# A per-sample convolution chain on one Trainium2 core: W in 18 product blocks, S2 on VectorE, the residual's identity on ScalarE, and R's shared products moved between W's

## The chip, the core and the metric

The kernel runs on one core of one Trainium2 chip. Its engines run side by side, each with its own instruction queue: TensorE (PE in the profile, its weight loads PEld) multiplies, VectorE (DVE), ScalarE (ACT) and GpSimd (POOL) work element by element, SyncE (SP) issues transfers. Products land in PSUM, eight banks of 512 fp32 columns on each of 128 partitions; everything else lives in SBUF. The metric is device time in microseconds, the median of several runs.

## The reference

A chain of four modulated 1-D convolutions, each with 64 channels in and out and three taps, on 128 samples of length 1024, and the input added at the end. Each sample has its own weights: a style vector scales the input channels, and a demodulation factor normalises the output channels.

```
s = style @ mw.T + mb
weight = SCALE * w * s[:, None, :, None]
demod = lax.rsqrt(jnp.sum(weight * weight, axis=(2, 3)) + EPS)
weight = weight * demod[:, :, None, None]
# types: 'same', 'upsample' (transposed conv, then blur), 'same', 'downsample' (blur, then stride 2)
...
x = x + _L0_cond_ref(x, cond_512, weights, biases, mod_w, mod_b)
```

Between the layers there is no nonlinearity, so for one sample the whole chain is one convolution of nine taps with a 64x64 matrix each, apart from a few columns at both ends.

## The kernel before, in words

**Tiling.** Samples are taken in 32 quads of four. A tile has 128 partitions, two samples of 64 channels, and two such halves. A "product" here is one weight block times one moving operand for all four samples: four 64x64 matmuls, one for each quarter of the array, which the profile records as 8 matmuls since each is fp32. A "block" is 64 columns.

**The chain for one quad.** scale3 makes wd (layer 3's weights, scaled per sample). stage1 multiplies by layer 2's weights and evicts S, scaled by table tB. stage2 multiplies by E (layer 1's taps with the blur) and evicts R, scaled by tC, seven blocks. stage3 multiplies by layer 0's weights and evicts W, nine blocks, scaled by t0. combine_a and combine_b on VectorE form sums of W (H, a fast-convolution scheme) and add the residual's identity to the middle tap (residual, L659). The input planes are combined alike into T. Then five convolutions, conv0 to conv4, each three groups of one 340-column product (L753), go into accumulator A (tile psA, two banks) or Y (two banks); VectorE combines them (sum1, sum2), ScalarE writes the output (L830), and SP stores it.

**Shared products.** From quad 8 on, parts of these products are computed once. stage1_a and stage1_b (L389) make S with w2n, negated taps and their sums, and VectorE's L442 and GpSimd's L445 complete it. share_sums (L462, VectorE) adds slots of S; share (L467, three products of one block) multiplies these by E into spare columns of accumulator A[q], and share_copy (L490, ScalarE) spreads them over psR, to which stage2_rest (L467, 14 products) adds. In stage3, r_sums (L588, GpSimd) adds slots of R; stage3_b (L571, 7 products into psA) ends with their product, ScalarE copies that into psW four times, and stage3_a (L571, 4 products into psW) adds the rest.

**Order.** The schedule is written by hand: each engine executes in program order. One turn q handles the convolutions of quad q, with n = q + 1, c = q + 2 and s = q + 4 in earlier stages: stage2(c), conv2(q), sum2(q), stage3_b(c), conv4(q), stage3_a(c), conv3(n), stage1_a(s), conv0(q), stage1_b(s), share(c + 1), conv1(n). Turns 0 to 3 have an order of their own (early_turn), turn 4 opens the shared form (entry), turns 5 to 28 are alike; share runs in turns 5 to 27 (sharing), and turns 10, 14, 15, 19 also carry products for the ends of the samples (SLOTS, L994). The last three quads follow in the open.

**PSUM.** All eight banks are in use: two accumulators psA of two banks (pool ps_conv), Y of two, and two single banks (pool ps_w) that psR, psW and psS take in turn; so each of these waits until the one before is evicted. In A, columns 0 to 339 of each bank hold the sums and the rest is spare; banks(q) names the two halves. sum2 is

```
m3 = m3c.pop(q)
for s, a in enumerate(banks(q)):
    sum_of(Y[:, s, :NB], m3[:, s], 3.0, a[:, :NB])
for s, a in parts(q) if 1 in steps else ():
    nc_v.tensor_sub(y1w[q][:, s], y1w[q][:, s], a)
```

that is, Y in two instructions (L662), and then y1 in one (L812), all reading A[q]. conv4 adds to Y and conv0 to A[q] afterwards. Small constants are computed in Y's spare columns; L1454 clears these.

Of the kernel before, what the change touches and what calls it, by code (L numbers as in the profile page):

```python
# [63 lines left out]
def kernel(  # L64
# [199 lines left out]
    def var_newton(bs, ls=slice(0, NL)):  # L264
# [5 lines left out]
    tA, tB, tBn, tC, t0, t3, td, tb = (  # L270
        const.tile([P, NQ, 2], F32, name=n) for n in ("tA", "tB", "tBn", "tC", "t0", "t3", "td", "tb")
# [24 lines left out]
    def table_Bn(bs):  # L296
        qs = slice(bs.start // 4, bs.stop // 4)
        nc_g.tensor_scalar_mul(tBn[:, qs], tB[:, qs], -1.0)

    def table_0(bs):  # L300
        table(nc_g, t0, bs, ALT, ODD, sc[:, 0, bs], 1.0)

# [63 lines left out]
    w2n = const.tile([P, 5, C], F32, name="w2n")  # L366

    def split_weights():
        nc_g.tensor_copy(w3x[:, :K], w3)
        nc_g.tensor_scalar_mul(w2n[:, :K], woi[2], -1.0)  # L370
        for t, src in ((w3x, w3), (w2n, woi[2])):
            nc_g.tensor_add(t[:, K:], src[:, : K - 1], src[:, 1:])
# [32 lines left out]
    EVEN = slice(0, K, 2)  # L405

    def stage1(q, pool=None, engs=(nc_a, nc_a), between=None):

        wd = chain[q]
        ps = unit(pool or ps_w, f"psS{q}")  # L410
        for k, (at, at1) in enumerate(((0, 3), (3, 1), (1, 4))):
            tap_matmul(ps, wd, at, 2, woi[2][:, k, :], EVEN, first=k == 0)
            tap_matmul(ps, wd, at1, 1, woi[2][:, k, :], slice(1, 2), last=k == K - 1)
        if between:
            between()
        st, _ = s_tiles(q)
        for r in range(2):
            scaled_copy(engs[r], flat(st[r][:, 1:6]), ps[r][:, : 5 * C], tB[:, q, r : r + 1])
        chain[q] = st
        return ps  # L420

    def stage1_a(q, ps=None):

        ps = ps or unit(ps_w, f"psS{q}")
        wd = chain[q]
        tap_matmul(ps, wd, 2, 2, w2n[:, 0, :], EVEN, first=True)
        tap_matmul(ps, wd, 3, 2, w2n[:, 2, :], EVEN)
        tap_matmul(ps, wd, 1, 1, w2n[:, 1, :], slice(1, 2))
        st, t = s_tiles(q)
        for r in range(2):  # L430
            scaled_copy(nc_a, flat(st[r][:, :4]), ps[r][:, C : 5 * C], tBn[:, q, r : r + 1])
        chain[q] = wd, ps, st, t

    def stage1_b(q):

        wd, ps, st, t = chain[q]
        tap_matmul(ps, wd, 2, 1, w2n[:, 3, :], slice(3, 4))
        tap_matmul(ps, wd, 4, 1, w2n[:, 4, :], slice(4, 5), last=True)
        for r in range(2):
            p1 = st[r][:, 0:1, :].to_broadcast([P, 2, C])  # L440
            sums = ps[r][:, 2 * C : 6 * C].rearrange("c (a b o) -> c a b o", a=2, b=2)[:, :, 0]
            nc_v.scalar_tensor_tensor(  # L442
                st[r][:, 4:6, :], sums, tB[:, q, r : r + 1], p1, op0=ALU.mult, op1=ALU.subtract
            )
        nc_g.tensor_add(t[:, :, 2], t[:, :, 2], t[:, :, 0])  # L445
# [7 lines left out]
    def tap_differences():  # L453
# [4 lines left out]
        nc_g.tensor_sub(Ed[:, 4:], E[:, 3:8:4], E[:, 5:6].to_broadcast([P, 2, C]))  # L458

    def share_sums(q):  # L460
        t = whole[q]
        nc_v.tensor_add(t[:, :, 6:8], t[:, :, 1:5:3], t[:, :, 2:6:3])  # L462
# [13 lines left out]
    def share(q, ps):  # L476

        at = [NB + 4 + i * C for i in range(3)]
        p12, p34 = ([b[:, i:j] for b in ps] for i, j in zip(at, at[1:]))
        chain_matmul(p12, E[:, 2], chain[q], slice(6, 7))  # L480
        chain_matmul(p34, E[:, 6], chain[q], slice(6, 7))
        chain_matmul(p34, E[:, 5], chain[q], slice(7, 8), True)
        shared_ps[q] = [b[:, at[0] : at[2]] for b in ps]

    def share_copy(q):

        ps = unit(ps_w, f"psR{q}")
        for r in range(2):
            src = shared_ps[q][r].rearrange("c (a o) -> c a o", a=2)
            nc_a.copy(  # L490
                ps[r][:, C : 5 * C].rearrange("c (a b o) -> c a b o", a=2, b=2),
# [4 lines left out]
    def stage2_rest(q):  # L496

        ps = shared_ps.pop(q)
        block = lambda i, n=1: [b[:, i * C : (i + n) * C] for b in ps]
        apart = [b[:, : 4 * C].rearrange("c (a b o) -> c a b o", a=2, b=2)[:, :, 0] for b in ps]  # L500
        plan = (
            (apart, E[:, 0], slice(1, 4, 2)),
            (block(1), Ed[:, 0], slice(2, 3)),
            (block(2), Ed[:, 1], slice(1, 2)),
            (block(3), E[:, 2], slice(3, 4)),
            (block(3), Ed[:, 2], slice(2, 3)),
            (block(4), Ed[:, 3], slice(1, 2)),
            (block(4), E[:, 4], slice(3, 4)),
            (block(5, 2), E[:, 8], slice(2, 4)),
            (block(5), E[:, 6], slice(3, 4)),  # L510
            (block(1, 2), E[:, 1], slice(4, 6)),
            (block(2), E[:, 3], slice(4, 5)),
            (block(3), Ed[:, 4], slice(5, 6)),
            (block(4), Ed[:, 5], slice(4, 5)),
            (block(5), E[:, 7], slice(5, 6)),
# [5 lines left out]
    def stage2(q, pool=None, engs=(nc_a, nc_a), between=None):  # L521
# [3 lines left out]
        for n, e in enumerate(() if shared else (-2, -1, 0, 1, 2, 3, 4, 5, 6)):  # L525
            if e % 2 == 0:
                a, lo, m = slice(1, 4), e // 2 + 1, 3
            else:
                a, lo, m = slice(4, 6), (e + 3) // 2, 2
            for r, rows in enumerate(HALF):  # L530
                for c, cols in enumerate(HALF):
                    src = st[c if r == 0 else 1 - c]
                    nc.tensor.matmul(  # L533
                        ps[r][cols, lo * C : (lo + m) * C],
                        E[rows, e + 2, :],
# [7 lines left out]
        t = r_pool.tile([P, 2, 9, C], F32, tag="R", name=f"R{q}")  # L543
        for r in range(2):
            scaled_copy(engs[r], flat(t[:, r, :7]), ps[r][:, : 7 * C], tC[:, q, r : r + 1])
# [4 lines left out]
    TAPS = slice(3, 9, 2), slice(4, 9, 2), slice(0, 3)  # L550

    def tap(kind, g):
        return range(9)[TAPS[kind]][g]
# [7 lines left out]
    def tap_shares():  # L561
        nc_g.tensor_sub(Wd[:, 0], woi[0][:, 0, :], woi[0][:, 1, :])
        nc_g.tensor_sub(Wd[:, 1], w0s[1][:, 2, :], w0s[1][:, 1, :])
# [16 lines left out]
    def stage3_out(q, ps, at, n, engs=(nc_a, nc_a)):  # L580
        W = Wq[q][0]
        for r in range(2):
            src = ps[r][:, : n * C].rearrange("c (a o) -> c a o", o=C)
            scaled_copy(engs[r], W[:, at : at + n, r], src, t0[:, q, r : r + 1])

    def r_sums(q, eng):
        t = chain[q]
        eng.tensor_add(t[:, :, 7:9], t[:, :, 2:6:3], t[:, :, 3:7:3])  # L588
# [3 lines left out]
    def stage3_b(q, ps):  # L592
# [16 lines left out]
        for i, f in enumerate((1.0, 1.0 / 3.0)):  # L609
            for dst, v in zip(blocks(pw, slice(i, i + 3, 2)), src):  # L610
                scaled_copy(nc_a, dst, v, f)
        stage3_out(q, ps, 0, 5)

    def stage3_a(q):
# [10 lines left out]
        stage3_out(q, pw, 5, 4)  # L625

    def stage3(q, part, pool=None, engs=(nc_a, nc_a)):
# [23 lines left out]
        stage3_out(q, ps, *((3, 6), (0, 3))[part], engs)  # L651
        return ps

    def residual(q):

        W = Wq[q][0]
        for r in range(2):
# [11 lines left out]
    def combine_a(q):  # L669
# [4 lines left out]
        residual(q)  # L674
# [91 lines left out]

# [870 lines left out]
```

## Time and profile before

| | |
|---|---|
| median of 3 runs | 480.74 us (480.36 to 481.32) |
| span of the profiled execution | 478.0 us |
| TensorE busy | 469.6 us, 98% |
| VectorE busy | 417.5 us, 87% |
| ScalarE busy | 310.1 us, 65% |
| GpSimd busy | 163.5 us, 34% |
| HBM traffic | 144 GB/s over the span |
| a turn without end products | 13.84 us |

The span runs from the first to the last instruction of one profiled execution, and the runs' time includes what lies around it. Engines overlap, so their times do not add up to the span. Rows of the profile give a line of the kernel (L753 is line 753; a line may be that of a helper), engine, operation, what is written and read, the shape, the count, the busy time and the mean of one in ns, and the idle time of the engine before it with what ended that.

### The profile page before, as it was taken

The page shows a single profiled execution, that of the slowest core. Times are in us where ns is not written, and L with a number is a line of the kernel's source. Part 1 is how long each engine was busy: PE and PEld are TensorE (multiplying, and loading weights), DVE is VectorE, ACT ScalarE, POOL GpSimd, SP SyncE. Part 2 cuts the span into 40 slices and gives each one's busy share as a digit, 9 for nine tenths or more (in the row PEclk, how much of TensorE's full clock was granted, in tenths as well). Part 3 has the DMA queues.
Part 4 walks back from the last instruction along what each step waited for, and adds up shares of the span by engine and source line. Part 5 has one row for each costly group of instructions (what it writes and reads, how often), then busy time and mean ns, then how long its engine had stood idle before and what let it go on. Part 6 is the DMA issues. An engine that isn't in the chain of part 4 may idle for free.

```text
span 478.0 us, 26721 instructions
## 1 busy us (share of the span) xinstructions
PE 469.6 (98%) x11928; PEld 346.4 (72%) x11928; DVE 417.5 (87%) x690; ACT 310.1 (65%) x708; POOL 163.5 (34%) x197
## 2 busy tenths in 40 slices
PE   8999999999999999999999999999999999999995
PEld 7877788777878876677776677766887777766652
DVE  5889998879889998899979899979989999999895
ACT  5565666667666676666667666667666768766352
POOL 3434032663335342243432233422434432333200
PEclk9999999999999999999999999999999999999998
DMA  5406365544445554345543455533455554445125
GB/s 175 158 28 200 114 195 192 150 139 144 139 150 157 173 173 127 122 151 160 171 149 120 131 170 152 173 127 126 145 169 162 162 154 146 152 146 170 61 91 191
DMA packets 50514, 70.70 MB, mean 148 GB/s; under 512 B 5664, under 2 KB 47328, under 8 KB 50400
## 3 DMA queue, kind: packets, MB, share of 16 engines
q1 hardware_dynamic: 49808, 68.32, 45.8%
q8 instruction: 93, 1.52, 1.5%
q10 hardware_dynamic: 592, 0.69, 0.5%
q14 instruction: 21, 0.17, 0.1%
HBM read 35.36 MB, written 33.62 MB: 144 GB/s over the span
## 4 chain that ended last, share of the span: by engine, by line
PE 95%; DVE 4%; issue 0%; ACT 0%; ACTq 0%; DVEq 0%
PE psA L753 45%; PE Y L753 11%; PE psR L467 9%; PE psA L571 7%; PE psW L571 7%; PE psS L389 6%; PE psR L533 4%; PE psA L467 2%; PE Y L994 2%; DVE H L662 1%; PE Y L180 1%; PE Y L336 1%; DVE G L662 0%; PE psM L204 0%; DVE o L832 0%
## 5 line engine op out<-in xcount | busy, mean ns | idle before, releaser
L753 PE MATMUL psA<-T,H 64*64 64x340 f32 x2304 | 187.3, 447 | 0.8 <-DVE y L662 0.7
L753 PEld LDWEIGHTS psA<-T,H 64*64 64x64 f32 x2304 | 89.9, 133 | 50.0 <-issue 3.1
L662 DVE SCALAR_TENSOR_TENSOR G<-X 128x1376 f32<-128x1376 f32 (+2 forms) x65 | 78.1, 1207 | 1.1 <-DMA X<-in_x 0.9
L726 POOL TENSOR_TENSOR T<-G 128x684 f32<-128x684 f32 x28 | 46.5, 1659 | 73.1 <-DVE G L662 73.1
L445 POOL TENSOR_TENSOR S<-S 128x128 f32<-128x128 f32 x28 | 22.1, 790 | 144.1 <-ACT S L360 136.8
L360 ACT ACTIVATE R<-psR,tC 128x448 f32<-128x448 f32 x63 | 36.5, 630 | 46.3 <-PE psR L467 26.7
L753 PE MATMUL psA<-T,Wf 64*64 64x340 f32 x768 | 63.9, 446 | 0.0
L753 PE MATMUL Y<-T,Wf 64*64 64x340 f32 x768 | 62.8, 451 | 0.1
L662 DVE SCALAR_TENSOR_TENSOR Y<-m,psA 128x340 f32<-128x340 f32 x64 | 33.1, 517 | 28.0 <-PE psA L753 26.6
L360 ACT ACTIVATE psW<-psA 128x128 f32<-128x128 f32 x100 | 19.3, 269 | 50.3 <-PE psA L571 46.2
L740 DVE TENSOR_TENSOR T<-G 128x1368 f32<-128x1368 f32 (+1 forms) x33 | 50.7, 1540 | 0.0
L360 ACT ACTIVATE Wf<-psW,t 128x256 f32<-128x256 f32 (+2 forms) x76 | 32.7, 479 | 26.5 <-PE psW L571 26.2
L711 DVE TENSOR_TENSOR T<-X 128x684 f32<-128x684 f32 x32 | 47.9, 1496 | 0.0
L467 PE MATMUL psR<-S,E 64*64 64x64 f32 (+1 forms) x1472 | 46.5, 238 | 0.0
L731 POOL TENSOR_TENSOR T<-G 128x684 f32<-128x684 f32 x28 | 46.5, 1660 | 0.0
L389 PEld LDWEIGHTS psS<-wd,w2n 64*64 64x64 f32 x1120 | 35.0, 133 | 13.3 <-ACT S L360 0.8
L467 PEld LDWEIGHTS psR<-S,E 64*64 64x64 f32 x1472 | 39.6, 134 | 5.2 <-ACT psR L490 0.2
L753 PEld LDWEIGHTS Y<-T,Wf 64*64 64x64 f32 x768 | 29.6, 132 | 18.0 <-DVE Y L662 0.7
L830 ACT ACTIVATE o<-psA,tb,td 128x340 f32<-128x340 f32 x63 | 37.0, 647 | 6.3 <-PE psA L753 6.3
L753 PEld LDWEIGHTS psA<-T,Wf 64*64 64x64 f32 x768 | 29.1, 133 | 15.1
L830 ACT ACTIVATE o<-Y,tb,td 128x340 f32<-128x340 f32 x63 | 36.6, 637 | 4.5 <-PE Y L753 2.7
L830 ACT ACTIVATE o<-y,tb,td 128x340 f32<-128x340 f32 x62 | 38.5, 679 | 0.6 <-DVE y L812 0.6
(165 smaller groups left out, 832.4 us busy)
## 6 DMA issues: line engine op xcount, KB each, us to landing
out<-o SPq DMA_DIRECT2D x167, 170.0 KB, 2.6
X<-in_x SPq DMA_DIRECT2D x150, 172.0 KB, 3.6
X<-in_x SPq DMA_DIRECT2D x14, 516.0 KB, 5.3
out<-o SPq DMA_DIRECT2D x6, 510.0 KB, 5.4
out<-o SPq DMA_DIRECT2D x2, 340.0 KB, 3.0
Xe<-in_x_ends SPq DMA_DIRECT2D x1, 512.0 KB, 6.7
out<-o ACTq DMA_DIRECT2D x3, 170.0 KB, 2.3
par<-in_params SPq DMA_DIRECT2D x2, 192.0 KB, 3.4
```

The source lines that it names most:

```text
L360: nc_a.activation(dst, src, AF.Copy, scale=f)
L389: nc.tensor.matmul(ps[r][cols, at * C : (at + n) * C], weight[rows], wd[c if r == 0 else 1 - c][rows, taps], start=first, stop=last, skip_ ...
L445: nc_g.tensor_add(t[:, :, 2], t[:, :, 2], t[:, :, 0])
L467: nc.tensor.matmul(dst[r][cols], weight[rows], st[c if r == 0 else 1 - c][rows, slots, :], start=False, stop=last, skip_group_check=True,)
L571: nc.tensor.matmul(dst[r][cols], weight[rows], t[rows, c, slots, :], start=first, stop=last, skip_group_check=True,)
L662: nc_v.scalar_tensor_tensor(out, x, f, y, op0=ALU.mult, op1=op)
L711: nc_v.tensor_sub(t[:, pairs, 0, :NJ], plane(X, 3, pairs), plane(X, 1, pairs))
L726: eng.tensor_add(t[:, :, 0, :NJ], plane(g, 2), plane(g, 1))
L731: eng.tensor_sub(t[:, :, 1, :NJ], plane(g, 2), plane(g, 1))
L740: nc_v.tensor_sub(t[:, pairs, :, :NJ], both(a, PL), both(b, 1))
L753: nc.tensor.matmul(ps[s][cols, :NB], w, Ts[q, tag][rows, c, i, g : g + NB], start=(g == 0 and m == 3), stop=(g == K - 1), skip_group_check ...
L830: nc_a.activation(dst, src, AF.Identity, bias=add, scale=d3)
```

## The change

In words:

- **W.** r_sums adds three pairs of R's slots instead of two (in two instructions on GpSimd, one for each half). stage3_b now has three products of one block, one of three, and one into psW; ScalarE spreads the shared three blocks over six of psW in two copies, and evicts two of W's blocks. stage3_a has three products of three blocks and one of two. All use layer 0's plain weights, and W's factors per kind of tap (1, 1/3, -2) are put into the eviction's scale (t0, t0b, t0c), so psW is evicted in six parts. W's slots are reordered.
- **S.** The sign moves from w2n and tBn to En, negated odd taps of E. S's slots are reordered; in the turns VectorE's stage1_b writes three slots, S2 among them, and GpSimd's addition is left out. The plain stage1 has three products of three blocks instead of six.
- **Residual.** In turns 5 to 28, identity makes t3 times the identity on ScalarE, and residual is one addition on VectorE.
- **Shared products of R.** share(c + 1) moves from behind stage1_b into the next turn's stage3_b (as its `between`), ahead of the last product into psA, and so behind sum2; share_sums moves to the end of the turn before. psR is shifted by one block, and stage2_rest takes the blocks that nothing is shared for first.
- **Accumulator.** A's sums take columns 172 to 851 of the two banks in one run, with 172 spare columns ahead and 172 behind; share writes there. sum2 in the turns makes Y in one instruction.
- **Order.** scale3(s) stands behind R's eviction instead of at the end of the turn before; copy_m3(n) comes directly behind conv3, conv0's first third ahead of stage1_a, outputs(q, 2) behind it, outputs(q, 1) behind share_copy; in turns with SLOTS two thirds of conv1 come ahead of these.

The core of the diff:

```diff
+    def table_0_kinds():
+        for t, f in ((t0b, 1.0 / 3.0), (t0c, -2.0)):
+            nc_g.tensor_scalar_mul(t, t0, f)
...
+    def negated_taps():
+        nc_g.tensor_scalar_mul(En, E[:, 1:8:2], -1.0)
...
-        for k, (at, at1) in enumerate(((0, 3), (3, 1), (1, 4))):
-            tap_matmul(ps, wd, at, 2, woi[2][:, k, :], EVEN, first=k == 0)
-            tap_matmul(ps, wd, at1, 1, woi[2][:, k, :], slice(1, 2), last=k == K - 1)
+        plain.add(q)
+        for k in range(K):
+            tap_matmul(ps, wd, k, K, woi[2][:, k, :], slice(0, K), first=k == 0, last=k == K - 1)
...
-    def stage1_b(q):
+    def stage1_b(q, eng=nc_v):
...
+            at = slice(3, 6, 1 if eng is nc_v else 2)
+            sums = blocks(ps, at)[r]
...
-        nc_g.tensor_add(t[:, :, 2], t[:, :, 2], t[:, :, 0])
+        if eng is not nc_v:
+            eng.tensor_add(t[:, :, 4], t[:, :, 4], t[:, :, 0])
...
     def share_sums(q):
         t = whole[q]
-        nc_v.tensor_add(t[:, :, 6:8], t[:, :, 1:5:3], t[:, :, 2:6:3])
+        nc_v.tensor_add(t[:, :, 1:8:6], t[:, :, 2:4], t[:, :, 4:6])
...
     def share(q, ps):
 
-        at = [NB + 4 + i * C for i in range(3)]
+        at = [i * C for i in range(3)]
...
     def r_sums(q, eng):
         t = chain[q]
-        eng.tensor_add(t[:, :, 7:9], t[:, :, 2:6:3], t[:, :, 3:7:3])
+        for r in (slice(0, 2),) if eng is nc_v else PAIR:
+            eng.tensor_add(t[:, r, 7:10], t[:, r, 0:6:2], t[:, r, 1:7:2])
...
-    def stage3_b(q, ps):
+    def stage3_b(q, ps, between=None):
...
-            (slice(0, 3), w0s[2][:, 2, :], slice(0, 7, 3)),
-            (slice(0, 2), w0s[2][:, 1, :], slice(1, 5, 3)),
-            (slice(0, 2), w0s[2][:, 0, :], slice(2, 6, 3)),
-            (slice(3, 4), w0s[0][:, 0, :], slice(0, 1)),
-            (slice(4, 5), w0s[1][:, 0, :], slice(1, 2)),
-            (slice(4, 5), w0s[1][:, 1, :], slice(0, 1)),
-            (slice(5, 7), w0s[0][:, 1, :], slice(7, 9)),
+            (slice(3, 4), w0s[1][:, 2, :], slice(5, 6)),
+            (slice(3, 4), w0s[1][:, 1, :], slice(6, 7)),
+            (slice(4, 5), w0s[2][:, 2, :], slice(6, 7)),
+            (slice(0, 3), woi[0][:, 1, :], slice(7, 10)),
         )
         for i, (at, weight, slots) in enumerate(plan):
+            if between and i == len(plan) - 1:
+                between()
             same_row(blocks(ps, at), weight, t, slots, i == 0, i == len(plan) - 1)
         pw = shared_w[q] = unit(ps_w, f"psW{q}")
-        src = blocks(ps, slice(5, 7))
-        for i, f in enumerate((1.0, 1.0 / 3.0)):
-            for dst, v in zip(blocks(pw, slice(i, i + 3, 2)), src):
-                scaled_copy(nc_a, dst, v, f)
-        stage3_out(q, ps, 0, 5)
+        same_row(blocks(pw, slice(0, 1)), woi[0][:, 0, :], t, slice(0, 1))
+        for r in range(2):
+            src = ps[r][:, : K * C].rearrange("c (a o) -> c a o", o=C)
+            dst = pw[r][:, C : 7 * C].rearrange("c (a b o) -> c a b o", b=2, o=C)
+            nc_a.copy(dst, src[:, :, None, :].to_broadcast([P, K, 2, C]))
+        for r, src in enumerate(blocks(ps, slice(3, 5))):
+            scaled_copy(nc_a, Wq[q][0][:, 7:9, r], src, t0[:, q, r : r + 1])
...
-            (slice(0, 3, 2), Wd[:, 0], slice(3, 7, 3)),
-            (slice(0, 3, 2), w0s[0][:, 2, :], slice(1, 5, 3)),
-            (slice(1, 4, 2), Wd[:, 1], slice(2, 6, 3)),
-            (slice(1, 2), w0s[1][:, 0, :], slice(4, 5)),
+            (slice(1, 6, 2), Wd[:, 0], slice(1, 6, 2)),
+            (slice(2, 7, 2), Wd[:, 1], slice(0, 5, 2)),
+            (slice(2, 7, 2), woi[0][:, 0, :], slice(2, 7, 2)),
+            (slice(3, 6, 2), woi[0][:, 2, :], slice(1, 4, 2)),
...
-        stage3_out(q, pw, 5, 4)
+        for kind, scale in enumerate((t0, t0b, t0c)):
+            at = slice(kind, 7, K)
+            for r, src in enumerate(blocks(pw, at)):
+                scaled_copy(nc_a, Wq[q][0][:, at, r], src, scale[:, q, r : r + 1])
...
+    def identity(q):
+        for r in range(2):
+            nc_a.activation(x3[:, r], idn3, AF.Copy, scale=t3[:, q, r : r + 1])
+
+    def residual(q, made):
 
         W = Wq[q][0]
+        if made:
+            v = W[:, tap(1, 1)]
+            nc_v.tensor_add(v, v, x3)
+            return
...
-        return [(slice(0, 2), A[q][:, :, :NB])]
+        both = flat(A[q])[:, SPARE : SPARE + 2 * NB]
+        return [(slice(0, 2), both.rearrange("c (s j) -> c s j", s=2))]
...
+    def spare(q):
+        return [flat(A[q])[:, i : i + SPARE] for i in (0, SPARE + 2 * NB)]
...
-            for s, a in enumerate(banks(q)):
-                sum_of(Y[:, s, :NB], m3[:, s], 3.0, a[:, :NB])
+            whole = parts(q) if wide else [(s, a[:, :NB]) for s, a in enumerate(banks(q))]
+            for s, a in whole:
+                sum_of(Y[:, s, :NB], m3[:, s], 3.0, a)
...
         stage2(c)
+        if not entry:
+            identity(n)
+            if s < NQ:
+                scale3(s)
...
-        stage3_b(c, open_a(n))
+        stage3_b(c, open_a(n), (lambda: share(c + 1, spare(q))) if sharing(q) else None)
...
         conv3(n)
+        copy_m3(n)
         if entry:
-            copy_m3(n)
-        outputs(q, 2)
+            outputs(q, 2)
+        else:
+            conv0(q, 0)
         if s < NQ:
             stage1_a(s)
         if not entry:
-            copy_m3(n)
+            outputs(q, 2)
         in04(n)
-        if sharing(q):
-            share_sums(c + 1)
...
         if sharing(q):
-            share(c + 1, banks(q))
             share_copy(c + 1)
+        if not entry:
+            outputs(q, 1)
         outputs(q, 0)
         if q in SLOTS:
             matmuls, width, rest = SLOTS[q]
+            conv1(n, 0, 1)
...
         sum1(n)
+        if sharing(q + 1):
+            share_sums(s)
...
-        if s + 1 < NQ:
-            scale3(s + 1)
```

More of the change, by code (lines that the diff above doesn't have):

```diff
@@ L269 @@
     ALT, ODD, DOWN = slice(0, 4, 2), slice(1, 4, 2), (slice(3, 4), slice(1, 2))
-    tA, tB, tBn, tC, t0, t3, td, tb = (
-        const.tile([P, NQ, 2], F32, name=n) for n in ("tA", "tB", "tBn", "tC", "t0", "t3", "td", "tb")
+    tA, tB, tC, t0, t0b, t0c, t3, td, tb = (
+        const.tile([P, NQ, 2], F32, name=n) for n in ("tA", "tB", "tC", "t0", "t0b", "t0c", "t3", "td", "tb")
     )
@@ L673, in combine_a @@
         sum_of(h1, c, -2.0, a)
-        residual(q)
+        residual(q, made)
         sum_of(h3, h1, 1.0 / 6.0, b)
@@ L765 @@
     m3c, y1w = {}, {}
+    SPARE = 512 - NB
     def parts(q):
@@ L779, in open_a @@
         A[q] = ps_conv.tile([P, 2, 512], F32, tag="u", name=f"psA{q}")
-        return banks(q)
+        return [A[q][:, s] for s in range(2)]
     def conv3(q, pool=None):
@@ L869 @@
     idn3 = const.tile([P, C], F32, name="idn3")
+    x3 = const.tile([P, 2, C], F32, name="x3")
     def scaled_weights():
@@ L1324, in early_turn @@
         stage2(c)
-        sum2(q)
+        sum2(q, wide=False)
         if q == 0:
@@ L1390, in early_turn @@
         else:
-            stage1_b(s)
+            stage1_b(s, nc_g)
         conv0(q, 2)
@@ L1396, in early_turn @@
         if twice:
-            stage1_b(s)
+            stage1_b(s, nc_g)
         if q == 0:
@@ L1417, in turn_of @@
         stage2(c)
+        if not entry:
+            identity(n)
+            if s < NQ:
+                scale3(s)
         if entry:
-            sum2(q)
+            sum2(q, wide=False)
             conv4(q)
@@ L1454, in turn_of @@
             nc_v.memset(high(bs.stop - bs.start), 0.0)
-        conv0(q, *((2,) if entry else range(K)))
+        conv0(q, *((2,) if entry else (1, 2)))
         if entry:
             conv1(n, 0, 1)
-        outputs(q, 1)
+            outputs(q, 1)
         if s < NQ:
@@ L1474, in turn_of @@
             small(q)
-        conv1(n, *((2,) if entry else range(K)))
+        conv1(n, *((2,) if entry or q in SLOTS else range(K)))
         sum1(n)
+        if sharing(q + 1):
+            share_sums(s)
         in3(c)
@@ L1494 @@
     stage3(c, 0)
-    sum2(q, (0,))
+    sum2(q, (0,), False)
     combine_a(n)
@@ L1515 @@
     conv2(n)
-    sum2(n, (0,))
+    sum2(n, (0,), False)
     combine_b(c, (1,))
@@ L1540 @@
     conv0(q, 1, 2)
-    sum2(n)
+    sum2(n, wide=False)
     for i in range(2):
```

124 lines of the change are left out of this document (65 added, 59 removed).

## The prediction

> **What bounds the kernel now.** I read the page's busy line and chain first, then one turn in the chain of waits, then the same turn in the timeline.
>
> ```profile
> span 478.0 us, 26721 instructions
> PE 469.6 (98%) x11928; PEld 346.4 (72%) x11928; DVE 417.5 (87%) x690; ACT 310.1 (65%) x708; POOL 163.5 (34%) x197
> PE 95%; DVE 4%; issue 0%; ACT 0%; ACTq 0%; DVEq 0%
> 200.75:214.59 13.84, 13.84 (x398) 9.79 (x394) 12.34 (x19) 9.78 (x24) 4.79 (x5) 1.00 0.50 156
> ```
>
> The last line is a window over one turn (length, then busy time of PE, weight loads, DVE, ACT, POOL, the granted clock): TensorE is busy for the whole 13.84 us at full clock, the others are not. So the time is the sum of TensorE's products plus whatever makes it wait. One turn in the chain of waits (start, length, what):
>
> ```profile
> 206.70 1.33 PE psA L571 x56
> 208.03 1.80 PE Y L753 x24
> 209.83 0.77 PE psW L571 x32
> 210.60 1.72 PE psA L753 x24
> 212.32 0.55 PE psS L389 x24
> 212.87 1.72 PE psA L753 x24
> 214.59 0.23 PE psS L389 x16
> 214.82 0.35 PE psA L467 x24
> 215.17 1.72 PE psA L753 x24
> 216.89 1.93 PE psR L467 x112
> 218.82 1.72 PE psA L753 x24
> ```
>
> In order: stage3_b, conv4, stage3_a, conv3, stage1_a, conv0, stage1_b, share, conv1, stage2, conv2. Two rows give the prices of one product (8 records): share is three products one block (64 columns) wide, 0.35/3 = 0.117 us; stage1_a is two of two blocks and one of one, so two blocks cost (0.55 - 0.117)/2 = 0.217. stage3_b is one of three, three of two and three of one: three blocks cost 1.33 - 0.65 - 0.35 = 0.33. conv4 takes 1.80 where every other convolution takes 1.72: 0.08 us in it is a wait.
>
> **W's products.** Before: 7 in stage3_b and 4 in stage3_a (three of two blocks, one of one), 19 blocks, 1.33 + 0.77 = 2.10 us. After: stage3_b has three of one block, one of three, and one of one into psW, 4 x 0.117 + 0.33 = 0.80; stage3_a three of three and one of two, 3 x 0.33 + 0.217 = 1.21. Sum 2.01: 0.09 less, all of it on the path, in 25 turns: -2.3 us. The new stage3_a writes every other block of psW.
>
> ```profile
> L571 PE MATMUL psW<-R,wsq 64*64 64x128 f32 x400 | 20.6, 269 | 0.0
> L571 PE MATMUL psA<-R,par 64*64 64x128 f32 x200 | 11.7, 272 | 0.6 <-issue 0.5
> ```
>
> The first of these already writes alternate blocks, the second two adjacent ones: 269 and 272 ns, so a stride of a block costs nothing and I add nothing. The Trainium skill (PSUM — Partial Sum Buffer, Specifications) says that a non-contiguous access pattern slows matmuls significantly; it gives no factor, and if such products took twice as long the sum would be 25 x 1.2 = 30 us higher, as an estimate by that page; the trace disagrees.
>
> **The shared products' new place.** This step decides. Before, share writes the accumulator's spare columns when nobody else is using that accumulator: after conv0, before outputs(q, 0) reads it. After, it stands in stage3_b, behind three narrow products, right after conv2; and sum2, which precedes it in the program, makes VectorE read both banks of that same accumulator twice, once for Y (L662) and once for y1 (L812).
>
> ```profile
> 206.52 0.94 PE L571 MATMUL psA<-R,w0s 64*64 64x192 f32 x24
> 206.77 1.07 DVE L662 SCALAR_TENSOR_TENSOR Y<-m,psA 128x340 f32<-128x340 f32 x2 [1.02 <-PE psA L753]
> 207.74 0.86 DVE L812 TENSOR_TENSOR y<-y,psA 128x680 f32<-128x680 f32 x1
> 207.89 1.35 PEld L753 LDWEIGHTS Y<-T,Wf 64*64 64x64 f32 x24
> 98.54 1.17 ACT L830 ACTIVATE o<-Y,tb,td 128x340 f32<-128x340 f32 x2
> 99.80 0.14 DVE L1454 MEMSET Y<- 128x96 f32 x1 [1.65 <-ACT o L830]
> ```
>
> Does a write to other columns wait for such a read? The last two rows answer: the memset at L1454 writes columns 344 to 439 of Y's second bank; ACT reads columns 0 to 339 of Y's banks until 98.54 + 1.17 = 99.71. No column is shared, yet the memset sat 1.65 us and began 0.09 after. So the program orders engines in an accumulator by something coarser than columns. conv4 shows it is no finer than the tile: its first products need Y's first bank alone, but its weight load at 207.89 follows the end of both sums (206.77 + 1.07 = 207.84). Putting the accumulator's two halves side by side (172 to 851) leaves both in the banks where share writes, so it frees nothing.
>
> The wait: Y becomes one instruction of 680 columns. I price it by the next row, the same operation at 680 columns into SBUF: 0.86, taken as 0.87 since this one writes PSUM.
>
> ```profile
> L662 DVE SCALAR_TENSOR_TENSOR y<-psA,m 128x680 f32<-128x680 f32 x32 | 27.6, 862 | 7.4 <-PE psA L753 5.9 <-PE psW L571 1.3
> ```
>
> It starts 206.77 and ends 207.64; L812 begins 0.10 before that end, as it does now, and ends 207.54 + 0.86 = 208.40; TensorE's load follows 0.05 later, 208.45. Without a wait share would start at 206.52 + 3 x 0.117 = 206.87. That is 1.58, and about 0.05 for a first load that can't run ahead (half of conv4's 0.08): 1.63 us in each turn. Queued behind it on TensorE are stage3_b's last product, psW's first, conv4 and all the rest; nothing else can run there. In exchange conv4's 0.08 goes, since Y is long done; r_sums is done too. Bounds: 1.5 (a faster wide read) to 1.75 (a slower one). sharing(q) holds for q = 5 to 27, 23 turns.
>
> **Evictions on ScalarE.** W used to take 4 small copies into psW and 4 evictions, 2 of five blocks and 2 of four. Now: 2 copies of 384 columns into psW, 2 evictions of 128, then 6 (two of 192, four of 128), and identity adds 2 of 64.
>
> ```profile
> 210.70 0.84 ACT L360 ACTIVATE Wf<-psW,t 128x256 f32<-128x256 f32 x2 [0.93 <-PE psW L571]
> L360 ACT ACTIVATE Wf<-psW,t 128x192 f32<-128x192 f32 x13 | 4.8, 418 | 0.4 <-PE psW L571 0.3 <-PE Y L914 0.2
> L360 ACT ACTIVATE psW<-psA 128x128 f32<-128x128 f32 x100 | 19.3, 269 | 50.3 <-PE psA L571 46.2
> ```
>
> The six take between 6 x 0.27 = 1.6 and 2 x 0.42 + 4 x 0.37 = 2.3 us, against 0.84. They must be out before stage1_a takes psS in the same banks. Between lie conv3 and, moved forward, conv0(q, 0), a third of 1.72: 2.29 us. The gap from product to eviction is 0.1 (210.60 to 210.70). I take 1.8: covered by 0.4, price nothing; were conv0's third not there it would cost 0.2. At the upper end it costs 0.1 to 0.2 a turn. stage1_b adds into columns that S's eviction reads; that cover shrinks from 1.72 to 1.15 against the same 0.84 for two of 256 columns, and 0.1: price 0, at worst 0.1. identity (at most 0.27 each, the 128-column row) and scale3 now follow R's eviction; psW's copies, which come behind them, are due later than now because share waits, so nobody is held. outputs(q, 2) and its two stores on SP move behind stage1_a, some 2 us later; only later stores stand behind them there. ScalarE gains 1.0 (six for two), 0.5 (identity), less 0.4 (128 for 320 columns): about 1.1 on 9.78, in a turn that becomes 15.3 long.
>
> **VectorE and GpSimd.** Y in one piece saves 0.2; the residual's two (304 ns each) become one add of 128 columns, bounded by the rows below at 0.28 to 0.42; S2's two grow from 128 to 192 columns, 0.07 each. VectorE is off the path; 0 us. GpSimd loses L445 and has two r_sums of 192 columns in place of one of 256, 1.1 to 1.5 us from R's eviction on, ready before share's wait ends.
>
> ```profile
> L659 DVE SCALAR_TENSOR_TENSOR Wf<-idn,t,Wf 128x64 f32<-128x64 f32 x64 | 16.9, 304 | 0.0
> L462 DVE TENSOR_TENSOR S<-S 128x256 f32<-128x256 f32 x23 | 9.6, 418 | 0.0
> L588 POOL TENSOR_TENSOR R<-R 128x256 f32<-128x256 f32 x24 | 17.7, 737 | 35.1 <-ACT R L360 35.1
> ```
>
> **The rest.** stage1 has 3 products of three blocks for 6 (0.99 for 1.00), 4 times; stage2's reordering, conv1's two thirds ahead of the slots, scaled tables: 0. The store and load triggers on SP keep their order and shift with their releasers. Turn 28 has no share: there conv4 has 0.80 of cover for Y, which ends 1.12 after stage3_b's start: +0.3. Two turns hold a gap in stage3_b that no engine explains:
>
> ```profile
> 122.11 0.13 PEld L571 LDWEIGHTS psA<-R,par 64*64 64x64 f32 x1 [0.77 <-issue]
> 193.26 0.21 PEld L571 LDWEIGHTS psA<-R,w0s 64*64 64x64 f32 x8 [0.56 <-issue]
> ```
>
> They lie where the new wait stands, and would hide in it: -1.2.
>
> **Sum.** 23 x (1.63 - 0.08 - 0.09) = 33.6; turns 4 and 28: -0.2 + 0.3; gaps -1.2: +32.5 us. On the profiled execution 478.0 + 32.5 = 510.5; the median of the runs stands 2.7 above that span (480.74), so 513.2; I say 513.
>
> **Rivals.**
> - *share does not wait* (the other side: faster). If the order is kept by columns, share runs at 206.87 beside VectorE's reads; W's saving remains (-2.3), conv4 has 0.80 + 0.35 of cover against Y's 1.12 + 0.05 and keeps its 0.08: 478.4. For it: the two ranges share no column. Against: the memset's 1.65 us. It decides at one point, whether share's first load stands at 0.35 or 1.9 us after stage3_b's start. The Trainium skill (PSUM — Partial Sum Buffer, PSUM bank collisions raise a hardware error) says that two engines in one bank at once get wrong data, not a stall, and that order has to be kept by bank; the memset agrees, and by that page this rival falls. I give it 0.13.
> - *share waits for Y alone*, if y1's read is not counted: load at 207.69, 0.82 + 0.05, so 23 x 0.70 = 16 less 1: 496. Against: L812 reads the same banks. 0.05.
> - *the six evictions also hold stage1_a, or S's hold stage1_b*, 0.1 to 0.25 a turn on top, 25 turns: 516 to 519. For it: the upper end of 2.3 us. 0.09.
> - The forecast: 0.73, its own range 509 to 516 by the bounds of the wait (23 x -0.13 and +0.12, and 1 below for a gap more or less).
>
> **Numbers.** 0.2%, about 1 us, is what a measurement of this kernel tells from no change. The forecast, the second and the third rival are slower: 0.87; the first is faster, 0.12, with 0.01 for no difference. The range takes the forecast and the evictions, with a margin below for other gaps hidden by the wait: 506 to 519, which leaves out 0.18.
>
> **What would show it.** Right: turns of 15.3 us; TensorE near 467/510 = 92% busy; at the head of the waits share's load in psA, ended by VectorE's y subtraction, 23 times 1.5 us or so; conv4 at 1.72; W's products at 0.80 and 1.21. Wrong: TensorE still at 98% with share unhindered (the first rival), a wait ended by Y's sum (the second), or waits of psS's loads on ScalarE (the third).

## The result, and the profile after

| | before | after |
|---|---|---|
| median of the runs (us) | 480.55 (480.25 to 481.32) | 521.08 (519.14 to 521.36) |
| span of the profiled execution (us) | 478.0 | 517.4 (its time 519.14) |
| ratio after to before, 95% interval | | 1.0843 (1.0813 to 1.0872) |

The change makes the kernel 8.4% slower. The prediction said 513.0 us with a range of 506 to 519: the sign and the mechanism came as forecast, the size is 8 us above it and outside the range. The page of the changed kernel first: span, busy time by engine, and the chain's shares.

```profile
span 517.4 us, 25798 instructions
PE 472.0 (91%) x11432; PEld 342.6 (66%) x11432; DVE 421.9 (82%) x642; ACT 341.7 (66%) x806; POOL 165.4 (32%) x198
PE 84%; DVE 12%; ACT 2%; issue 1%; ACTq 0%; DVEq 0%
```

TensorE is busy for about as long as before (472.0 against 469.6 us) in a span 39.4 us longer. So the new time is time in which it stands, and VectorE, which held 4% of the chain before, holds 12%. Three rows of the list of waits say where it stands (engine, waiting instruction, what ended the wait: us in all, times, longest):

```profile
PEld psA L477 <- DVE y L849: 37.9, 23, 2.6
...
DVE cc L968 <- ACT o L867: 6.1, 2, 3.3
DVE oc L964 <- ACT o L867: 3.3, 1, 3.3
```

The first row is the forecast's: the shared products' weight load into the accumulator (L477), held 23 times by VectorE's subtraction for y1 (L849). The last two are new too; nothing in the prediction stands for them. The chain over one steady turn (start, length, what):

```profile
219.75 0.87 DVE Y L690
220.62 0.78 DVE y L849
...
221.44 0.58 PE psA L477 x24
222.02 0.33 PE psA L582 x8
222.34 0.11 PE psW L582 x8
222.46 1.72 PE Y L781 x24
224.18 1.19 PE psW L582 x32
```

conv2 ends at 219.66. VectorE reads the accumulator twice, from 219.75 on, and only then does share run; stage3_b's last product, psW's first, conv4 and stage3_a stand behind it. Three narrow products and share would have ended 0.70 later, at 220.36; they ended at 222.02. The wait is 1.66 (1.63 in the prediction). conv4 takes 1.72, without its stall of before. W's products take 0.35 + 0.33 + 0.11 + 1.19 = 1.98 (2.01 predicted). Most turns now last 15.34 us (15.3 predicted) instead of 13.84. One window over turns 5 to 8 and one over turn 14, before and then after (length; busy PE, PEld, DVE, ACT, POOL; granted clock), show where that isn't all:

```profile
101.44:158.88 57.44, 56.91 (x1509) 45.93 (x1508) 51.49 (x83) 39.82 (x95) 24.09 (x35) 1.00 0.52 155
230.55:246.11 15.56, 15.56 (x412) 11.22 (x408) 14.29 (x23) 11.27 (x27) 6.38 (x5) 1.00 0.49 153
```
```profile
100.88:167.71 66.83, 57.70 (x1445) 43.11 (x1445) 52.10 (x75) 43.69 (x108) 23.45 (x35) 1.00 0.42 126
246.46:266.18 19.72, 17.27 (x396) 11.56 (x392) 14.21 (x20) 12.83 (x31) 5.97 (x5) 0.91 0.40 126
```

Turns 5 to 8 grew by 9.4 us where the prediction's steps give 5.1 (4 x 1.46 less a gap of 0.77), and turn 14 by 4.2 instead of 1.5. Those two stretches hold the difference between the spans; the rest of the kernel came within 0.5 us of the sum.

**Turns 5 to 8.** The timeline of ScalarE, VectorE and (after) TensorE in turn 5, first before and then after (start, length, engine, line; in brackets the idle time ahead and what ended it):

```profile
110.78 1.16 ACT L830 ACTIVATE o<-Y,tb,td 128x340 f32<-128x340 f32 x2
113.75 0.25 DVE L930 TENSOR_TENSOR cc<-Y,a 128x96 f32<-128x96 f32 x1
```
```profile
114.30 0.84 ACT L361 ACTIVATE S<-psS,tB 128x256 f32<-128x256 f32 x2 [0.34 <-PE psS L394]
115.03 1.16 ACT L867 ACTIVATE o<-Y,tb,td 128x340 f32<-128x340 f32 x2
116.22 0.26 DVE L968 TENSOR_TENSOR cc<-Y,a 128x96 f32<-128x96 f32 x1 [2.77 <-ACT o L867]
117.07 0.30 PE L1277 MATMUL Y<-cc,wsum 64*64 64x96 f32 x2 [1.44 <-DVE Y L1496]
```

The change put outputs(q, 2), ScalarE's read of Y, behind stage1_a and so behind S's evictions. In turns 5 to 7 VectorE reads small constants out of Y's spare columns; in 5 and 6 it then clears them, and TensorE puts the next ones there (L1277). Before, ScalarE had left Y at 111.94, well ahead of that step. Now VectorE's step sits 2.77 us until 116.19, TensorE stands 1.44 for its small product, and everything queued on VectorE behind the step (S2, two sums) comes late to the next turn's share.

**Turn 14.** The chain into turn 14 of the changed kernel, and two windows behind it:

```profile
245.37 0.41 DVE S L451
245.78 1.50 DVE G L690
247.28 0.78 DVE y L690
248.05 1.33 DVE S L472
249.38 0.78 DVE T L739
250.16 0.68 DVE g L1004
...
251.41 0.86 DVE Y L690
...
253.09 0.58 PE psA L477 x24
...
254.51 3.00 PE Y L781 x24
```
```profile
253.00:257.50 4.50, 4.41 (x69) 2.72 (x72) 4.34 (x8) 1.39 (x4) 0.00 (x0) 0.62 0.34 118
257.50:260.00 2.50, 2.50 (x59) 1.79 (x52) 0.87 (x1) 1.20 (x5) 0.00 (x0) 1.00 0.03 7
```

VectorE works without a break from S2 on, with the shared products' sums (S L472, moved here) and two setup steps of turn 13's end (g L1004) in the row, and starts Y 1.2 us after conv2 has ended. TensorE then stands for 2.5 us. And when it goes on, it is slow: conv4 takes 3.00 instead of 1.72, the granted clock is 0.62 over 4.5 us and 1.00 afterwards.

### The profile page after: what moved, and what is told of

It is laid out like the page before. It is cut to its first block, busy times and chain, and to the rows that moved or that the text cites. A ratio compares the mean times of both kernels' runs of the same rounds, so it can differ in the third digit from the quotient of the medians.

```text
span 517.4 us, 25798 instructions
## 1 busy us (share of the span) xinstructions
PE 472.0 (91%) x11432; PEld 342.6 (66%) x11432; DVE 421.9 (82%) x642; ACT 341.7 (66%) x806; POOL 165.4 (32%) x198
## 4 chain that ended last, share of the span: by engine, by line
PE 84%; DVE 12%; ACT 2%; issue 1%; ACTq 0%; DVEq 0%
PE psA L781 39%; PE Y L781 10%; PE psW L582 9%; PE psR L477 8%; PE psS L394 5%; DVE Y L690 4%; PE psR L544 4%; DVE y L849 4%; PE psA L477 3%; PE psA L582 2%; PE Y L1032 2%; DVE G L690 1%; ACT o L867 1%; DVE y L690 1%; DVE S L472 1%
## 5 line engine op out<-in xcount | busy, mean ns | idle before, releaser
L781 PE MATMUL psA<-T,Wf 64*64 64x340 f32 x768 | 67.7, 446 | 0.0
L361 ACT ACTIVATE Wf<-psW,t 128x192 f32<-128x192 f32 (+1 forms) x76 | 30.1, 445 | 43.8 <-PE psW L582 43.5
L627 ACT COPY psW<-psA 128x384 f32<-128x384 f32 x50 | 21.2, 467 | 50.7 <-PE psW L582 47.0
L451 DVE SCALAR_TENSOR_TENSOR S<-psS,tB,S 128x192 f32<-128x192 f32 (+1 forms) x56 | 20.1, 400 | 42.2 <-PE psS L394 42.2
L690 DVE SCALAR_TENSOR_TENSOR H<-Wf 128x384 f32<-128x384 f32 x64 | 45.9, 717 | 0.0
L604 POOL TENSOR_TENSOR R<-R 128x192 f32<-128x192 f32 x48 | 38.7, 827 | 16.1 <-ACT R L361 16.0
L477 PE MATMUL psA<-S,E 64*64 64x64 f32 x368 | 10.6, 230 | 34.7 <-DVE y L849 34.7
L690 DVE SCALAR_TENSOR_TENSOR Y<-m,psA 128x680 f32<-128x680 f32 (+1 forms) x40 | 29.1, 728 | 15.2 <-PE psA L781 14.9
L781 PEld LDWEIGHTS psA<-T,Wf 64*64 64x64 f32 x768 | 27.7, 133 | 16.2
L690 DVE SCALAR_TENSOR_TENSOR H<-H,Wf 128x384 f32<-128x384 f32 x64 | 35.9, 561 | 2.2
```

The costliest lines, as they stand in the source:

```text
L361: nc_a.activation(dst, src, AF.Copy, scale=f)
L477: nc.tensor.matmul(dst[r][cols], weight[rows], st[c if r == 0 else 1 - c][rows, slots, :], start=False, stop=last, skip_group_check=True,)
L604: eng.tensor_add(t[:, r, 7:10], t[:, r, 0:6:2], t[:, r, 1:7:2])
L627: nc_a.copy(dst, src[:, :, None, :].to_broadcast([P, K, 2, C]))
L690: nc_v.scalar_tensor_tensor(out, x, f, y, op0=ALU.mult, op1=op)
L781: nc.tensor.matmul(ps[s][cols, :NB], w, Ts[q, tag][rows, c, i, g : g + NB], start=(g == 0 and m == 3), stop=(g == K - 1), skip_group_check ...
```

## The experiments

Each is named by its label; the ratios are to the kernel before, beside which it ran.

### The shared products back in their old place

```
-        stage3_b(c, open_a(n), (lambda: share(c + 1, spare(q))) if sharing(q) else None)
+        stage3_b(c, open_a(n))
...
         if sharing(q):
+            share(c + 1, spare(q))
             share_copy(c + 1)
```

> The changed kernel with one thing undone: the shared products stand behind stage1_b again, just ahead of their copy, as in the kernel before; W's products, the accumulator's layout, the evictions and the sums all stay as changed. Theory (the shared products' wait for VectorE's two reads of their accumulator is the loss): the waits of 1.5 us in 23 turns go, and with them VectorE's lateness in turn 14 and the low clock behind it; steady turns back at 13.8 us, the time 479 to 483 us, the upper end if the extra waits of turns 5 to 8 stay. Rival (the other edits cost time too: more evictions on ScalarE, VectorE's longer tail at a turn's end): steady turns above 14.2 us, the time 488 us or more.

Measured: 490.56 us, ratio 1.0212 (1.0192 to 1.0232). Against the changed kernel's 521.08 the place is worth 30.5 us of the loss, but neither forecast holds whole: the total is the rival's, and the steady turns are 14.14, between the theory's 13.8 and the rival's 14.2 and 0.3 above before. Stage3_b and conv4 in the chain of one such turn, and the waits of the whole run:

```profile
225.56 0.88 PE psA L582 x27
...
226.82 1.76 PE Y L781 x24
```
```profile
PEld psA L582 <- POOL R L604: 4.4, 13, 0.6
PEld Y L781 <- DVE Y L690: 3.7, 13, 0.7
```

stage3_b takes 1.26 instead of 0.80, and conv4 starts when Y's read has ended. With its work shortened to 0.80 and no wait in it, stage3_b outruns two things that used to lie beside it: GpSimd's sums of R, now two instructions, and VectorE's read of Y (0.87 and the start after conv2). Y's read decides when conv4 starts: in each of turns 5 to 28 conv4's first load comes about 0.05 us after that read ends, whether GpSimd's sums ended 0.5 us after its start or 0.2 before it. But in 11 of these 24 turns the late sums keep stage3_b going until then, so that a quicker read by itself would bring little there; no run separates the two. These 0.3 us are the cost that the prediction gave to turn 28 alone, where no share stands in between (14.41 against 14.12, +0.3 as predicted), and that the wait for share hides in the other turns. So the change has a second loss underneath the first.

### The place alone, in the kernel before

```
-        stage3_b(c, open_a(n))
+        stage3_b(c, open_a(n), (lambda: share(c + 1, banks(q))) if sharing(q) else None)
...
-            share(c + 1, banks(q))
             share_copy(c + 1)
...
         sum1(n)
+        if sharing(q + 1):
+            share_sums(s)
```

> The kernel before with one thing done: the shared products stand in stage3_b ahead of its last product, and their sums at the end of the turn ahead. There stage3_b still has its seven products, so the shared ones come 1.11 us after its start instead of 0.35. Theory: they wait until both reads of VectorE are done, 2.08 us after that start, about 0.97 + 0.05 us less conv4's 0.08: 23 x 0.94 = 22 us more than before, 500 to 505 us. Rival (the loss comes from the accumulator's layout or from W's new products, not from the place): 480 to 483 us.

Measured: 503.23 us, ratio 1.0491 (1.0463 to 1.0519), +23.3; steady turns 14.83, +0.99.

```profile
PEld psA L467 <- DVE y L814: 21.3, 23, 1.4
```

The same wait, shorter by as much as stage3_b's six products ahead of share are longer than the three of the changed kernel. Neither the accumulator's new layout nor W's new products are needed for it.

### The second read behind the shared products

```
-            sum2(q)
+            sum2(q, (0,))
...
+        if not entry:
+            sum2(q, (1,))
```
(the added lines stand behind stage3_b)

> The changed kernel with the sum for y1 put behind stage3_b and its shared products in the program's order, so that these follow Y's read alone. Theory (both reads count, one after the other): the wait falls from 1.55 by the 0.78 us of the second read, 23 x 0.78 = 18 us less than the changed kernel, 501 to 504 us, the wait ended by Y's sum. Rival (the wait is for something that ends with y1 by chance, such as the sum's buffer or VectorE's queue as a whole): 519 to 521 us.

Measured: 501.26 us, ratio 1.0446 (1.0418 to 1.0475); steady turns 14.58, 0.76 less than the changed kernel's.

```profile
PEld psA L477 <- DVE Y L690: 20.6, 23, 1.8
...
DVE y L849 <- PE psA L477: 16.1, 23, 0.7
```

The wait is now ended by Y's read, and the second read waits for TensorE in its turn. The second read counts for its own length, as the forecast had it (0.78).

### The shared products first, the sums behind

```
-            sum2(q)
-            in2(n, nc_g)
...
         stage3_b(...)
+        if not entry:
+            sum2(q)
+            in2(n, nc_g)
```

> The changed kernel with the shared products where the change put them on TensorE, but VectorE's two sums behind stage3_b in the program's order, so that VectorE waits for TensorE instead. Theory (the order of the two accesses is kept by the whole accumulator, whichever comes first): no wait of the shared products; Y's read starts when they end, 0.70 us after stage3_b's start, and ends 0.92 later, against conv4 due at 1.15, which waits some 0.5: turns of 14.3 us, 492 to 498 us. Rival (the place itself costs, in the banks or in the queue, whatever the order): turns of 15 us or more, over 510 us.

Measured: 500.14 us, ratio 1.0418 (1.0397 to 1.0438); steady turns 14.48.

```profile
229.82 0.35 PE psA L582 x24
230.16 0.40 PE psA L477 x24
...
230.65 0.88 DVE Y L690
...
231.58 1.95 PE Y L781 x24
```

share runs in the same place without a wait: it is the program's order and not the place that holds it. Y's read begins 0.09 after share's end, 0.83 after stage3_b's start (0.70 expected), conv4 1.76 after it. The total is above the range that I gave: conv4 takes 1.95 instead of 1.72 when its first load can't run ahead, 0.23 that I had left out, and turn 5 lasts 17.66.

### Turn 13's setup steps later

```
-    LATE = {13: lambda: setup1(1)}
+    LATE = {}
...
         6: zeros,
+        14: lambda: setup1(1),
```
(the second table holds what stands behind sum2)

> The changed kernel with VectorE's two setup steps of turn 13's end (0.68 + 0.63 us) moved behind the sums of turn 14. Theory (in turn 14 VectorE came late, so the wait grew to 2.6 us, and after it TensorE had a granted clock of 0.6 to 0.7 for 4 us): turn 14 loses 1.2 us of wait and some 1.7 us of slow products, 19.7 to about 16.8 us, the time 518 us, granted clock 1.00 there. Rival (the clock's dip comes at a set time whatever the wait): 1.2 us less at most, the dip still there.

Measured: 517.28 us, ratio 1.0773 (1.0757 to 1.079), 3.8 under the changed kernel's median. Turn 14 lasts 17.06 instead of 19.72, 2.7 less.

```profile
250.28 0.87 DVE Y L690
...
252.99 1.72 PE Y L781 x24
```
```profile
252.00:256.50 4.50, 4.50 (x108) 3.31 (x112) 4.36 (x9) 1.89 (x6) 0.61 (x1) 1.00 0.69 208
```

Y's read starts on time, conv4 takes 1.72, the granted clock at 1.00 over the same products. With the long wait gone the dip is gone, at the same place in the kernel: it was a consequence of the wait.

### Third outputs ahead in turns 5 to 7

```
             conv0(q, 0)
+        if q in (5, 6, 7):
+            outputs(q, 2)
         if s < NQ:
             stage1_a(s)
-        if not entry:
+        if not entry and q not in (5, 6, 7):
             outputs(q, 2)
```

> The changed kernel, in turns 5, 6 and 7 alone with the third outputs (they read Y) ahead of S's evictions on ScalarE again, as in the kernel before. Theory (in these turns VectorE's step with the small constants, and through it TensorE's small product and the next turn's sums, wait for ScalarE to read Y, which the change put 1 to 2 us later): turns 5 to 8 lose 2 to 3.3 us together of the 9.3 that they are longer than before, 518 to 519 us. Rival (their excess comes from the shared products' sums on VectorE, or from GpSimd): 521 us, the turns as they were.

Measured: 517.72 us, ratio 1.0777 (1.0751 to 1.0803), 3.4 under the changed kernel's median and a little below the theory's 518. Turns 5, 6 and 8 lose 1.06, 1.16 and 0.56, turn 7 nothing: 64.0 together instead of 66.8, within the 2 to 3.3 us that the theory gave. Turn 14 stays at 19.5, with its low clock.

### Both at once, and what is left

The edit is the two diffs just shown, together, on the changed kernel.

> The changed kernel with both of the local edits at once: third outputs ahead in turns 5 to 7, and turn 13's two setup steps behind the sums of turn 14; the shared products stay in stage3_b. Theory (the account adds up: what is left over the kernel before is the shared products' wait, 23 x 1.5, and little else): 513 to 515 us, the value that the prediction's sum gave for the whole change; turn 14 at 17.1, turns 5 to 8 together at 64. Rival (the two places overlap, so that curing both gives no more than one): 516 to 517 us.

Measured: 515.37 us, ratio 1.0726 (1.0703 to 1.0749), just above the theory's range; turn 14 at 17.06, turns 5 to 8 at 64.0, span 513.5. In these turns of the profiled executions the two cures add up (2.7 + 2.8 = 5.5 us), so the places do not overlap; by the medians they give 5.7 where the two alone gave 7.2, and that difference isn't traced. What is left over the kernel before is 35.3 us: the prediction's whole sum was 32.5. Of the 2.8 between them, 23 x 0.04 = 0.9 is the steady turn's 1.50 instead of 1.46, and about 1.4 what turns 5 to 8 have beside that: they still grew by 6.6 where the prediction's steps give 5.1. The rest isn't traced.

### Both cures with the shared products back

The edit is the same two diffs and the first experiment's.

> The first experiment (shared products back behind stage1_b) with the two further edits: third outputs ahead in turns 5 to 7, and turn 13's two setup steps behind the sums of turn 14. Theory (its 10 us over the kernel before are 23 times 0.3 because conv4 has only the shortened stage3_b as cover for Y's read, and the rest lies in these places): 2 to 3 us less in turns 5 to 8 and 1.2 in turn 14, steady turns still 14.14, 486 to 488 us. Rival (all of it is spread over the turns, from ScalarE's more evictions): 490 us.

Measured: 489.25 us, ratio 1.0193 (1.0169 to 1.0218): above the theory's range and nearer to the rival's 490. Turns 5 to 8 lose 1.7 and turn 14 0.5, less than expected; a likely reason, not shown, is that lateness of VectorE costs less where share doesn't pass it on to TensorE. Steady turns stay at 14.14, so about 23 x 0.3 = 7 of the 9 us over the kernel before lie where the first experiment found stage3_b and conv4 waiting, for GpSimd's sums and for Y's read.

### The wide read of Y alone, in the kernel before

```
-            for s, a in enumerate(banks(q)):
-                sum_of(Y[:, s, :NB], m3[:, s], 3.0, a[:, :NB])
+            for s, a in parts(q):
+                sum_of(Y[:, s, :NB], m3[:, s], 3.0, a)
```

> The kernel before with Y read in one instruction of 680 columns instead of two of 340, and nothing else. Theory (conv4 waits for Y's read; here stage3_b's 1.33 us cover the 1.17 of the single read, but not the 1.32 of the two): conv4 at 1.72 instead of 1.80, 0.08 in 25 turns, 2 us less: 478 us. Rival (the 0.08 is a cost of the switch to Y's weights and not a wait): 480 us, conv4 still at 1.80.

Measured: 477.75 us, ratio 0.9954 (0.9932 to 0.9975): 0.5% faster than the kernel before, a small gain whose interval leaves out 1. Steady turns last 13.75, 0.09 less. Of the parts of the change it is the one tried alone that pays. It does so beside stage3_b's old 1.33 us, which cover the read; beside the new 0.80 (the first experiment) conv4 waits for it. W's products are shorter too, 1.98 against 2.10 us, but were not tried alone.

```profile
219.84 1.27 PE psA L571 x49
221.11 1.77 PE Y L753 x24
```

stage3_b and conv4 take 1.27 + 1.77 = 3.04 where they took 1.33 + 1.80 = 3.13 (the border between the two moves with the order of the records, the sum doesn't).

### The changed kernel once more

No edit.

> The changed kernel once more, for where its executions differ by 2 us (spans of 517.4 in the profiled one, 519.3 to 519.5 in three others). If it lies in TensorE's clock behind turn 14's wait: a span near 519.4 and a longer or a second stretch of low granted clock, all turns else as they were. If it lies in a VectorE or ScalarE wait that comes and goes: the stretch the same, and some of the turns 5 to 13 longer by 0.5 to 2 us.

Measured: one time of 520.38 us, span 518.6. Turn 14 lasts 19.55 with the same dip, and turns 5 to 13 are as they were. The 1.2 us more lie in turn 20 (15.76 for 15.33), turn 26 (15.75 for 15.45) and behind the last turn; in turn 20 the chain names it:

```profile
348.86 0.16 issue
```

These are small gaps on TensorE that no engine explains, in other places from one execution to the next. Neither of my two guesses was right. Why most executions of the changed kernel take 2 us more than the profiled one stays open.

## Why the prediction was right in its mechanism and wrong in its size

- **The shared products' wait**: right. 23 waits for VectorE's second read, 1.66 us in a steady turn (1.63 predicted). That the price fits so well is partly luck, since two errors cancel in it. The prediction counted share's undisturbed start from 206.52, the first record of stage3_b, while the chain has conv2 on TensorE until 206.70: counted from there, the reads hold share 1.40 us by the prediction's own times, and 1.43 were measured (221.44 less 219.66 and 0.35). And share's first load after the wait costs 0.23 (0.58 for 0.35) instead of the 0.05 that I allowed. The place alone, the second read taken away and the order turned round moved the turn by +0.99, -0.76 and -0.86, as such a wait has to.
- **W's products and conv4's stall**: right (1.98 us and 1.72), and so were turn 28 (+0.29, though GpSimd's sums hold stage3_b there too) and, of the two gaps, the one in turn 11, which grew by 0.97 instead of 1.50. The gap in turn 6 can't be read off, since that turn lost time elsewhere.
- **Evictions on ScalarE**: right for stage1_a and stage1_b; the third rival has no such waits over 0.5 us. But the same paragraph has the step that failed first: "outputs(q, 2) and its two stores on SP move behind stage1_a, some 2 us later; only later stores stand behind them there." I asked who waits for the stores on SP and not who else waits for ScalarE to leave Y. The row that answers was in the prediction itself, the memset at L1454 that waited 1.65 us for exactly that read; I used it as evidence for the order by accumulator, and not as a waiter on the moved step. It cost 2.8 us in turns 5 to 8 (3.4 by the medians).
- **"VectorE is off the path; 0 us"**: wrong. The step was true of the kernel before, where a late sum is met by conv4 behind 1.33 us of other work. The change itself puts share right behind the sums, and so every late start of VectorE straight onto TensorE. It also moves the sums for share into the stretch between S2 and Y. In turn 14 that row of VectorE's work is 1.2 us too long.
- **The clock**: missing from the sum. The 2.5 us of standing in turn 14 cut the granted clock, and the slow products behind it cost about as much as the wait's growth (conv4 alone 1.28). Together with the row above it is 2.7 us of turn 14 (3.8 by the medians).
- **The profiled execution**: I carried the sum from before's profiled execution to its median by 2.7 us. The changed kernel's profiled execution has 478.0 + 39.4; its other runs lie 2 us higher, and why stays open.
- **The first rival's price**: 478.4 us was for share beside the reads, where it would cover conv4. It doesn't hold for share in the old place, where 490.56 was measured.

## What to carry to other kernels

When a step is moved past another, list everything that waits for each of them, not only what waits for the queue that you have in view. "Off the path" is a property of the cover between an engine and the one that ends the turn: if an edit takes that cover away, or shortens the work that is the cover, every late step of that engine has a price again, the setup steps of single turns first. Of an edit with several parts, one that pays may be small and separable: here one instruction instead of two.

## What the runs showed of the hardware

- **Waits of 2.1 to 2.5 us halved TensorE's clock.** Stretches of 3.41 us: two of the changed kernel in turn 14, the first with the wait, then one with turn 14's wait in the run with third outputs ahead, and one with the longest wait of the run with the second read behind (length; busy PE, PEld, DVE, ACT, POOL; granted clock):

```profile
250.16:253.57 3.41, 0.96 (x56) 0.82 (x52) 3.38 (x7) 1.06 (x3) 2.83 (x3) 1.00 0.86 227
253.57:256.98 3.41, 3.41 (x44) 1.93 (x40) 3.31 (x6) 1.39 (x4) 0.00 (x0) 0.50 0.28 98
```
```profile
247.20:250.61 3.41, 1.59 (x40) 0.98 (x32) 3.38 (x6) 1.86 (x5) 3.37 (x3) 1.00 0.74 165
```
```profile
244.68:248.09 3.41, 1.73 (x72) 1.34 (x68) 2.68 (x4) 1.20 (x4) 2.69 (x3) 1.00 0.88 215
```

  In these traces' clock records the granted clock changes only at steps of 3.41 us, and apart from the start and the end of each span it fell in three traces only, those with turn 14 at 19.5 to 19.7 us, for one step each. In the steps just ahead of the falls TensorE stood for 2.45, 2.21 and 1.82 us (3.41 less 1.59, of a wait of 2.13). The most in any other step ahead of the last product was 1.68, in the last row, and there the clock stayed. So in these runs the clock fell behind a step in which TensorE stood for more than about half; no run was made to find the border. The Trainium skill (TensorE: Matmul & The Clock Gate, Part 1: The HAM clock gate) gives half and full as this gate's two states, and the trace agrees with 0.50 and 1.00; it puts the fall after at least one idle window of about 3.4 us, and here a wait of 2.1 us was enough.
- **VectorE stood while GpSimd read and wrote SBUF.** The sums for share took 418 ns in mid-turn before. In their new place 19 of the 23 run beside GpSimd's add for T and take 1.07 to 1.44 us. The other four, where GpSimd isn't adding, still take 0.41 to 0.42. One of each kind, and GpSimd's add beside the first:

```profile
232.63 1.43 DVE L472 TENSOR_TENSOR S<-S 128x256 f32<-128x256 f32 x1
```
```profile
348.71 0.41 DVE L472 TENSOR_TENSOR S<-S 128x256 f32<-128x256 f32 x1
```
```profile
232.11 1.67 POOL L754 TENSOR_TENSOR T<-G 128x684 f32<-128x684 f32 x1 [10.11 <-DVE G L690]
```

  Each of the 19 ends 0.28 us after GpSimd's add, which takes its usual 1.66. So most of their time is standing. The Trainium skill (SBUF — State Buffer, Who interferes with whom) calls the port pair that the two share an exclusive lock, and these rows agree.
- Whether two engines could use different columns of one accumulator at the same time wasn't tried: every kernel here keeps such an order. Nor does a run tell whether it is kept by the whole accumulator or bank by bank, since share writes both of its banks and VectorE reads both.
